# The feed-forward gate of a conditioned transformer block: half of the inner state copied out of PSUM beside the tanh and multiplied on GpSimd, and the attention's reciprocals kept in PSUM

## The chip, the cores and the metric

The kernel runs on one core of a Trainium2 chip. The metric is the device time of the whole program in microseconds. TensorE is written PE here, VectorE DVE, ScalarE ACT, GpSimd POOL, and SyncE, which issues the DMAs, SP. All data is fp32, except for a mask kept in bf16.

## The reference, cut to what matters

Eight sequences of 512 tokens, 256 channels wide, pass through an adaptive-norm transformer block with 16 heads of 16 channels and an additive attention bias, then an adapter with experts and a layer norm, a rotation of channel pairs, and a second adapter. The two places that the change touches:

```python
probs = jax.nn.softmax(scores, axis=-1)
ctx = jnp.einsum('bhqk,bhkd->bhqd', probs, v)
...
def _gelu2(x):
    return x * jax.nn.sigmoid(1.702 * x)
h = _ln(x) * g2 + beta2
ff = _gelu2(h @ W1 + b1) @ W2 + b2        # W1: 256 x 1024, W2: 1024 x 256
```

The kernel writes the sigmoid as a tanh: `sigmoid(1.702 z) = 0.5 * tanh(0.851 z) + 0.5`, with `z = h @ W1 + b1`. The softmax is normalised late: a column of ones beside each head's values gives the sum of the exponentials, and the context is multiplied by the sum's reciprocal.

## The kernel before, in words

Attention goes in 128 units, `(b, g, qt)`: one sequence, a group of four heads, 128 queries. Each unit loads four bias tiles of 128 x 512 by DMA (L909), and POOL adds the mask to each (L913). PE computes four tiles of scores into four PSUM banks (L921). DVE subtracts scores and bias and finds the row's extreme (L933), ACT takes the exp in place (L937). The probabilities are turned, half of them on PE (L972) with an eviction by ACT or DVE (L693), half on DVE (L948) with a DMA that puts the blocks in place (L957). After every second unit PE multiplies them with the values (L998) into a bank called `pv`.

From there DVE alone works: it transposes the 128 x 256 columns of `pv` into an SBUF tile `pvs` (L1011), takes the reciprocals of eight sums into an SBUF tile `inv` (L1020), multiplies the context by them into `zed` (L1021), and after two groups transposes that into `ctx` (L1028).

After eight units, half a sequence is finished (`finish`): the output projection, the feed-forward, two adapters. `feed_forward` takes 256 tokens at a time, and for the last half sequence of all 128 at a time. The 1024 inner channels go in eight chunks of 128, two to a group, so there are 68 groups in all, 60 of them 256 tokens wide. In each, PE writes two chunks into the two halves of one PSUM bank (L1053), ACT takes a tanh of each half into `sig` (L1062), POOL makes 0.5 t + 0.5 of both at once (L1065), and DVE multiplies that by the biased inner state, which it reads from the bank again (L1069). The product `gT` is the stationary operand of the second matmul (L1078).

The order of the work is not written by hand. Each step is a task with an engine and a cost, the buffers and tiles that it reads and writes, and a rank. `Plan.run` plays these tasks through in a model with their costs: a free engine takes the ready task of lowest rank. A task with costs for two engines goes to whichever is free, ACT first. What comes out is the order in which instructions are emitted, for PE, DVE, ACT, POOL and SP together; each engine then works through its own in that order, with semaphores between them. So a changed cost or dependency can shift the order of everything after it. Eight PSUM banks are split in two sets of four: `SC` for the scores, `BG` for all the rest, which may borrow from `SC`. There are 16 bias tiles, the room for four units.

```python
BG = Slots(banks[4:], SC)
BIAS = slots("bias", 16, [P, S])
GT = slots("gT", 1, [P, NF, 2 * P])
SIG = slots("sig", 2, [P, 2, 2 * P])
```

Of the kernel before, what the change touches and what calls it, by code (L numbers as in the profile page):

```python
# [11 lines left out]
F32 = mybir.dt.float32  # L12
# [3 lines left out]
AF = mybir.ActivationFunctionType  # L16
ALU = mybir.AluOpType
AX = mybir.AxisListType

P = 128  # L20
B, S, D, H, HD, FF = 8, 512, 256, 16, 16, 1024
# [3 lines left out]
NF = FF // P  # L25
# [13 lines left out]
C_BQ, C_BK, C_B1, C_G2, C_BETA2, C_DB, C_FREQ, N_COLS = 0, 4, 8, 16, 18, 20, 22, 23  # L39
# [5 lines left out]
PE, DVE, ACT, POOL, DMA = "PE", "DVE", "ACT", "POOL", "DMA"  # L45
# [193 lines left out]
def conditioned_sequence_kernel(  # L239
# [22 lines left out]
    nc = tc.nc  # L262
    const = ctx.enter_context(tc.tile_pool(name="const", bufs=1))
# [9 lines left out]
    def slots(name, count, shape, dtype=F32):  # L273
        return Slots([const.tile(shape, dtype, tag=f"{name}{i}", name=f"{name}{i}") for i in range(count)])
# [3 lines left out]
    BG = Slots(banks[4:], SC)  # L278
# [12 lines left out]
    PT = slots("pT", 2, [P, 4 * NT * 2 * P])  # L291
    TB = slots("tb", 2, [P, TURNED * S])
    PVS = slots("pvs", 2, [P, 2 * P])
    INV = slots("inv", 2, [P, 8])
    ZED = slots("zed", 2, [P, 8, 2, HD])
    CTX = slots("ctx", 2, [P, NC, 2 * P])
    HT = slots("hT", 2, [P, NC, 2 * P])
# [13 lines left out]
    cols = const.tile([P, N_COLS], F32, tag="cols", name="cols")  # L311
# [66 lines left out]
    plan = Plan()  # L378
# [8 lines left out]
    wq = const.tile([P, NC, NC, P], F32, tag="wq", name="wq")  # L387
    wk = const.tile([P, NC, NC, P], F32, tag="wk", name="wk")
    b1s = const.tile([P, NF], F32, tag="b1s", name="b1s")
    valid = const.tile([A, B], F32, tag="valid", name="valid")  # L390
    invalid = const.tile([A, B], F32, tag="invalid", name="invalid")
    expert_i = const.tile([1, B], I32, tag="expert_i", name="expert_i")
# [106 lines left out]
    def constants():  # L499
        plan.rank = -13.0  # L500

        further = Buffer(BG, lambda t: t[:, :8])
        plan(PE, 0.3, lambda: nc.tensor.matmul(
            further.t, shifted[:, :P], cols[:, :8], start=True, stop=True),
            [], [further], mode="full", at=3.9)

        def biases():
            nc.vector.tensor_tensor(
                bk,
                cols[:, C_BK : C_BK + NG].rearrange("p (c u) -> p c u", u=2)[:, :, 0],  # L510
                further.t[:, 4:8].rearrange("p (c u) -> p c u", u=2)[:, :, 1],
                ALU.add,
            )

            for u, src in enumerate((cols[:, C_BQ : C_BQ + NG], further.t[:, :4])):
                nc.vector.tensor_scalar(
                    bqh[:, u], src.rearrange("p (c u) -> p c u", u=2)[:, :, u],
                    halves[:, u : u + 1], None, ALU.mult,
                )

        plan(DVE, 0.6, biases, [further], ["bk", "bqh"], at=7.9)
        plan.rank = -1.9
        for n in (1, 2):
            plan(DMA, 0.45, lambda n=n: half_of(n, 1), [], [("raw", n, 1)], data=0.8)

        for c in range(NC):
            for n, w in ((1, wq), (2, wk)):

                def dense(n=n, w=w, c=c):
                    for k in range(NC):  # L530
                        src = first[:, n, k, c * 2 * P : (c + 1) * 2 * P]
                        src = src.rearrange("p (u j e) -> p u j e", u=2, e=32)[:, :, :, :HD]
                        dst = w[:, k, c, :].rearrange("p (j u d) -> p u j d", u=2, d=HD)
                        nc.gpsimd.tensor_copy(dst, src)

                plan.rank = -9.0 + 0.1 * n + 6.0 * c
                plan(POOL, 0.55, dense, [("raw", n, c)], [("w", n, c)], at=0 if c else 7.3 + 0.8 * n)


        for i, v_pad in enumerate(VP.tiles):  # L540

            def clear(v_pad=v_pad, i=i):
                nc.gpsimd.memset(v_pad, 0.0)
                ones = v_pad[:, : NT * H * (HD + 1)].rearrange("p (n e) -> p n e", e=HD + 1)
                nc.gpsimd.memset(ones[:, :, HD : HD + 1], 1.0)
                nc.gpsimd.memset(VT.tiles[i][:, NT * NG * TURNED * (HD + 1) :], 0.0)

            plan.rank = -10.0
            plan(POOL, 1.3, clear, [], [("ones", i)])
        plan.rank = 1.0  # L550

        def later():
            for hid in HID.tiles:
                nc.gpsimd.memset(hid[A:A1, :], 1.0)

        plan(POOL, 0.6, later, [], ["hid1"])

        plan(ACT, 0.25, lambda: nc.scalar.activation(
            b1s, cols[:, C_B1 : C_B1 + NF], AF.Copy, scale=0.851), [], ["b1s"], at=4.0)

    def late_weights():
        wo_rows = w_o.rearrange("(c u j e) n -> c j u e n", c=NC, u=2, e=32)
# [336 lines left out]
    def attention(u, n):  # L899
        b, g, qt = u  # L900
        c, par = divmod(g, 2)
        half, i = divmod(qt, 2)
# [64 lines left out]
        for j in range(turned, 4):  # L967
            ps = Buffer(BG, lambda t: t.rearrange("p (k q) -> p k q", k=NT))
# [15 lines left out]
        if g == 0:  # L984
            live[(b, half)] = Buffer(CTX)
        ctx_h = live[(b, half)]
        pv = Buffer(BG, lambda t: t[:, : 2 * P])

        def values():
            for kc in range(NT):  # L990
                for j in range(4):
                    at = ((j * NT + kc) * NG + g) * (HD + 1)
                    if j < turned:
                        pj = pT.t[:, : 8 * TURNED * P].rearrange(
                            "p (a h k c) -> p h k a c", a=8, h=TURNED, k=NT)[:, j, kc]
                    else:
                        pj = pT.t.rearrange("p (j k f) -> p j k f", j=4, k=NT)[:, j, kc]
                    nc.tensor.matmul(  # L998
                        pv.t[32 * j : 32 * j + 32, :],
                        (v_turn if j < turned else v_pad).t[:, at : at + 32],  # L1000
                        pj, start=(kc == 0), stop=(kc == NT - 1),
                    )
# [4 lines left out]
             + [(pT, a) for a in range(2) if turned], [pv], mode="col")  # L1007


        sb, inv = Buffer(PVS), Buffer(INV)  # L1010
        plan(DVE, 0.37, lambda: nc.vector.transpose(  # L1011
            sb.t.rearrange("p (i b c) -> p b i c", i=2, c=32),
            pv.t.rearrange("p (b i c) -> p b i c", i=2, c=32)), [pv], [sb])
        if par == 0:
            live[(b, half, c)] = Buffer(ZED)
        zed = live[(b, half, c)]

        def normalise():
            of = sb.t.rearrange("p (b e) -> p b e", e=32)
            nc.vector.reciprocal(inv.t, of[:, :, HD])  # L1020
            nc.vector.tensor_tensor(  # L1021
                zed.t[:, :, par, :], of[:, :, :HD],
                inv.t.unsqueeze(2).to_broadcast([P, 8, HD]), ALU.mult,
            )

        plan(DVE, 0.45, normalise, [sb], [inv, (zed, par)])
        if par == 1:
            plan(DVE, 0.35, lambda: nc.vector.transpose(  # L1028
                ctx_h.t[:, c, :], zed.t.rearrange("p b u d -> p (b u d)")),
                [(zed, 0), (zed, 1)], [(ctx_h, c)])  # L1030


    def feed_forward(res, rk, ts, store=None):
        hat = Buffer(TMP)
        at = {t: i for i, t in enumerate(ts)}
        n, w = len(ts), len(ts) * P
# [7 lines left out]
        gT = Buffer(GT) if store is None else store  # L1044
        for f2 in range(NF // 2):
            ps = Buffer(BG, lambda t: t.rearrange("p (i q) -> p i q", i=2))
            sg = Buffer(SIG)
            for i in range(2):
                f = 2 * f2 + i

                def hidden(i=i, f=f, ps=ps):
                    for c in range(NC):
                        nc.tensor.matmul(  # L1053
                            ps.t[:, i, :w], w1[:, c, f * P : (f + 1) * P], hT.t[:, c, :w],
                            start=(c == 0), stop=(c == NC - 1),
                        )

                plan(PE, 0.432 * n, hidden, [*hk, "w1"], [(ps, i)], mode="full")

            for i in range(2):  # L1060
                f = 2 * f2 + i
                plan(ACT, 0.155 + 0.1 * n, lambda i=i, f=f, ps=ps, sg=sg: nc.scalar.activation(  # L1062
                    sg.t[:, i, :w], ps.t[:, i, :w], AF.Tanh, bias=b1s[:, f : f + 1],
                    scale=0.851), [(ps, 0), (ps, 1), "b1s"], [(sg, i)])
            plan(POOL, 0.05 + 0.3 * n, lambda sg=sg: nc.gpsimd.tensor_scalar(  # L1065
                sg.t[:, :, :w], sg.t[:, :, :w], 0.5, 0.5, ALU.mult, ALU.add), [], [(sg, 0), (sg, 1)])
            for i in range(2):
                f = 2 * f2 + i
                plan(DVE, 0.14 + 0.13 * n, lambda i=i, f=f, ps=ps, sg=sg: nc.vector.scalar_tensor_tensor(  # L1069
                    gT.t[:, f, :w], ps.t[:, i, :w], cols[:, C_B1 + f : C_B1 + f + 1],  # L1070
                    sg.t[:, i, :w], ALU.add, ALU.mult), [(ps, i), (sg, i)], [(gT, f)])
        ps = Buffer(BG, lambda t: t.rearrange("p (i d) -> p i d", i=2))
        for i in range(n):
            for f0 in range(0, NF, 2):
# [317 lines left out]
```

## Time and profile before

| | |
|---|---|
| time of the runs | 930.76, 931.76, 935.42 us; median 931.76 |
| the profiled execution | 928.04 us, span 926.3 us |
| PE busy | 887.0 us, 96% of the span |
| DVE busy | 827.4 us, 89% |
| POOL busy | 755.3 us, 82% |
| ACT busy | 748.6 us, 81% |
| DMA engines, mean bandwidth | 236 GB/s |

The profile is of one execution. It counts an engine as busy while an instruction of its own runs; time in which an instruction waits at the head of its queue is idle time, and the profile names what ended it. Matmuls are pipelined, so PE can be shown as busy while it makes little progress. A row of the costliest groups gives the source line, the engine, the operation, output and inputs by name, their shapes, the count, and then the busy time in us, the mean duration of one in ns, and the idle time just before them with what ended it. A row of waits gives who waited for whom, the sum in us, how many times, and the longest.

### The profile page before, as it was taken

The page shows a single profiled execution, that of the slowest core. Times are in us where ns is not written, and L with a number is a line of the kernel's source. Part 1 is how long each engine was busy: PE and PEld are TensorE (multiplying, and loading weights), DVE is VectorE, ACT ScalarE, POOL GpSimd, SP SyncE. Part 2 cuts the span into 40 slices and gives each one's busy share as a digit, 9 for nine tenths or more (in the row PEclk, how much of TensorE's full clock was granted, in tenths as well). Part 3 has the DMA queues.
Part 4 walks back from the last instruction along what each step waited for, and adds up shares of the span by engine and source line. Part 5 has one row for each costly group of instructions (what it writes and reads, how often), then busy time and mean ns, then how long its engine had stood idle before and what let it go on. Part 6 is the DMA issues. An engine that isn't in the chain of part 4 may idle for free.

```text
span 926.3 us, 20595 instructions
## 1 busy us (share of the span) xinstructions
PE 887.0 (96%) x6430; PEld 576.8 (62%) x6430; DVE 827.4 (89%) x2197; ACT 748.6 (81%) x1357; POOL 755.3 (82%) x843
## 2 busy tenths in 40 slices
PE   9989999999999999999999999999998999999994
PEld 7546665656556666566656666566655666666682
DVE  4789888999989999989999998999998899999866
ACT  5976879878797778978889887987989779798653
POOL 8877999998687877998688887997879878999232
PEclk9999999999999998999999999999999999999997
DMA  9578786787867878787888869878796878998400
GB/s 316 172 242 271 233 266 194 219 275 246 290 174 245 264 218 283 213 266 244 244 263 246 283 204 288 246 227 270 235 310 197 258 250 274 290 301 263 108 23 23
DMA packets 163215, 218.55 MB, mean 236 GB/s; under 512 B 19167, under 2 KB 93961, under 8 KB 163106
## 3 DMA queue, kind: packets, MB, share of 16 engines
q1 hardware_dynamic: 163062, 217.22, 75.0%
q8 instruction: 51, 0.84, 0.4%
q14 instruction: 58, 0.48, 0.2%
q10 hardware_dynamic: 44, 0.02, 0.0%
HBM read 149.89 MB, written 4.24 MB: 166 GB/s over the span
## 4 chain that ended last, share of the span: by engine, by line
PE 51%; DVE 21%; ACT 12%; DMA 6%; issue 4%; POOL 3%; SPq 1%; DVEq 0%; POOLq 0%; ACTq 0%
PE bank L921 9%; PE bank L972 8%; PE bank L998 8%; PE bank L1078 7%; DVE bias L933 7%; PE bank L1053 6%; PE bank L811 5%; ACT bias L937 4%; DVE tb L948 3%; DMA pT<-tb 3%; DMA bias<-in_bias 3%; PE bank L759 2%; DVE st L701 2%; ACT sig L1062 1%; PE bank L410 1%
## 5 line engine op out<-in xcount | busy, mean ns | idle before, releaser
L913 POOL TENSOR_TENSOR bias<-bias,neg 128x512 f32<-128x512 f32 x512 | 582.0, 1164 | 84.8 <-DMA bias<-in_bias 57.1
L937 ACT ACTIVATE bias<-bias,low 128x512 f32<-128x512 f32 x512 | 341.9, 719 | 58.6 <-DVE low L933 57.6
L933 DVE CUSTOM_DVE_ANT_0 bias<-bank,bias 128x512 f32<-128x512 f32 x512 | 326.1, 679 | 21.2 <-PE bank L921 20.9
L972 PEld LDWEIGHTS bank<-shifted,bias 128*128 128x128 f32 x1120 | 126.1, 142 | 78.7 <-ACT bias L937 33.7
L972 PE MATMUL bank<-shifted,bias 128*128 128x128 f32 x1120 | 157.9, 280 | 12.7 <-DVE pT L693 5.1
L921 PE MATMUL bank<-kT,qz 32*128 32x512 f32 x1024 | 166.4, 642 | 1.5 <-DVE low L933 1.3
L948 DVE STREAM_TRANSPOSE tb<-bias 128x512 f32<-128x512 f32 x232 | 153.6, 689 | 10.8 <-DMA pT<-tb 6.3
L693 ACT COPY pT<-bank 128x512 f32<-128x512 f32 x221 | 121.4, 584 | 40.5 <-PE bank L972 39.6
L1053 PE MATMUL bank<-hT,w 128*128 128x256 f32 (+1 forms) x544 | 126.9, 375 | 0.5 <-DVE gT L1069 0.2
L998 PE MATMUL bank<-pT,v_pad 128*32 128x256 f32 x1120 | 124.3, 385 | 0.0
L1078 PE MATMUL bank<-w,gT 128*128 128x256 f32 x496 | 118.5, 384 | 0.5 <-DVE pT L693 0.3
L998 PE MATMUL bank<-pT,v_turn 128*32 128x256 f32 x928 | 112.7, 385 | 2.8 <-DMA pT<-tb 1.6
L1053 PEld LDWEIGHTS bank<-hT,w 128*128 128x128 f32 x544 | 93.8, 190 | 30.4 <-issue 12.2
L1078 PEld LDWEIGHTS bank<-w,gT 128*128 128x128 f32 x496 | 90.4, 190 | 25.5 <-issue 12.1
L921 PEld LDWEIGHTS bank<-kT,qz 32*128 32x128 f32 x1024 | 50.9, 183 | 54.2 <-issue 26.6
L998 PEld LDWEIGHTS bank<-pT,v_turn 128*32 128x32 f32 x928 | 50.2, 110 | 52.5 <-issue 9.8
L1065 POOL TENSOR_SCALAR sig<-sig 128x512 f32<-128x512 f32 (+1 forms) x68 | 40.3, 594 | 32.5 <-ACT sig L1062 29.0
L1062 ACT ACTIVATE sig<-bank,b1s 128x256 f32<-128x256 f32 (+1 forms) x136 | 55.1, 455 | 11.7 <-PE bank L1053 11.2
L998 PEld LDWEIGHTS bank<-pT,v_pad 128*32 128x32 f32 x1120 | 55.0, 110 | 5.9 <-ACT bias L937 1.5
L1069 DVE SCALAR_TENSOR_TENSOR gT<-bank,cols,sig 128x256 f32<-128x256 f32 (+1 forms) x128 | 53.8, 462 | 3.1 <-POOL sig L1065 2.8
L701 DVE BATCH_NORM_STATS2 st<-res 128x6 f32<-128x256 f32 x128 | 52.1, 407 | 1.6 <-DMA res<-in_x 0.2
L1021 DVE TENSOR_TENSOR zed<-pvs,inv 128x128 f32<-128x128 f32 x64 | 49.0, 766 | 2.2
(138 smaller groups left out, 1127.4 us busy)
## 6 DMA issues: line engine op xcount, KB each, us to landing
bias<-in_bias SPq DMA_DIRECT2D x512, 256.0 KB
pT<-tb SPq DMA_DIRECT2D x464, 128.0 KB
out<-res SPq DMA_DIRECT2D x15, 256.0 KB
res<-in_x SPq DMA_DIRECT2D x7, 512.0 KB
v_turn<-v_pad SPq DMA_DIRECT2D x32, 68.0 KB
m<-in_mask SPq DMA_DIRECT2D x8, 256.0 KB
mod<-ada_rows SPq DMA_DIRECT2D x8, 256.0 KB
w<-in_w SPq DMA_DIRECT2D x2, 1024.0 KB
```

The source lines that it names most:

```text
L693: nc.scalar.copy(*pair()) if e == ACT else nc.vector.tensor_copy(*pair())), r, w)
L701: plan(DVE, 0.43, lambda t=t, st=st: nc.vector.bn_stats(st.t, src.t[:, t, :]), [key], [st], at=at[i] if at else 0.0)
L913: plan(POOL, 1.12, lambda j=j: nc.gpsimd.tensor_tensor(dif[j].t, dif[j].t, negs[qt].t, ALU.add), [negs[qt]], [dif[j]])
L921: nc.tensor.matmul(sc[j].t, qz.t[strip, par, c, qs], kT.t[strip, c, :], start=True, stop=True,)
L933: plan(DVE, 0.61, lambda j=j: nc.vector.tensor_tensor_reduce(dif[j].t, sc[j].t, dif[j].t, -1.0, 3.0e38, ALU.add, ALU.min, low.t[:, j : j + ...
L937: plan(ACT, 0.61, lambda j=j: nc.scalar.activation(dif[j].t, dif[j].t, AF.Exp, bias=low.t[:, j : j + 1], scale=-1.0), [(low, j)], [dif[j]] ...
L948: plan(DVE, 0.62, lambda j=j: nc.vector.transpose(tb.t.rearrange("p (m h k c) -> h p k m c", m=4, h=TURNED, k=NT)[j], dif[j].t.rearrange(" ...
L972: nc.tensor.transpose(ps.t[:, kc, :], dif[j].t[:, kc * P : (kc + 1) * P], ident)
L998: nc.tensor.matmul(pv.t[32 * j : 32 * j + 32, :], (v_turn if j < turned else v_pad).t[:, at : at + 32], pj, start=(kc == 0), stop=(kc == N ...
L1053: nc.tensor.matmul(ps.t[:, i, :w], w1[:, c, f * P : (f + 1) * P], hT.t[:, c, :w], start=(c == 0), stop=(c == NC - 1),)
L1062: plan(ACT, 0.155 + 0.1 * n, lambda i=i, f=f, ps=ps, sg=sg: nc.scalar.activation(sg.t[:, i, :w], ps.t[:, i, :w], AF.Tanh, bias=b1s[:, f : ...
L1078: nc.tensor.matmul(ps.t[:, i, :], gT.t[:, f, i * P : (i + 1) * P], w2[:, f, :], start=(f == 0), stop=(f == NF - 1),)
```

## The change

Two edits.

In the attention, the reciprocals no longer have an SBUF tile. They go into eight unused columns of the `pv` bank, from where the multiplication reads them; the task that does so now holds the bank as well, so that it comes free one task later. Three planned costs of DVE in this part are raised a little.

In the feed-forward, a second pass over the bank is added for each chunk: 0.5 z, out of PSUM into `gT`, by ACT or by DVE as the planner finds (`half_out`); for this `b1h` holds half the bias. POOL's step becomes t + 1, and POOL multiplies it by 0.5 z in place, two chunks at a time. The product on DVE, L1069, is gone, and so is its second reading of the bank after POOL.

```diff
-    INV = slots("inv", 2, [P, 8])
...
+        plan(ACT, 0.25, lambda: nc.scalar.activation(
+            b1h, cols[:, C_B1 : C_B1 + NF], AF.Copy, scale=0.5), [], ["b1h"], at=4.0)
...
-        pv = Buffer(BG, lambda t: t[:, : 2 * P])
+        pv = Buffer(BG)
...
-        sb, inv = Buffer(PVS), Buffer(INV)
-        plan(DVE, 0.37, lambda: nc.vector.transpose(
+        sb = Buffer(PVS)
+        plan(DVE, 0.43, lambda: nc.vector.transpose(
...
-            nc.vector.reciprocal(inv.t, of[:, :, HD])
+            inv = pv.t[:, 2 * P : 2 * P + 8]
+            nc.vector.reciprocal(inv, of[:, :, HD])
             nc.vector.tensor_tensor(
-                zed.t[:, :, par, :], of[:, :, :HD],
-                inv.t.unsqueeze(2).to_broadcast([P, 8, HD]), ALU.mult,
+                zed.t[:, :, par, :], inv.unsqueeze(2).to_broadcast([P, 8, HD]),
+                of[:, :, :HD], ALU.mult,
             )
 
-        plan(DVE, 0.45, normalise, [sb], [inv, (zed, par)])
+        plan(DVE, 0.52, normalise, [sb, pv], [(pv, "inv"), (zed, par)])
...
+                def half_out(e, i=i, f=f, ps=ps):
+                    if e == ACT:
+                        nc.scalar.activation(
+                            gT.t[:, f, :w], ps.t[:, i, :w], AF.Identity,
+                            bias=b1h[:, f : f + 1], scale=0.5)
+                    else:
+                        nc.vector.tensor_scalar(
+                            gT.t[:, f, :w], ps.t[:, i, :w], cols[:, C_B1 + f : C_B1 + f + 1],
+                            0.5, ALU.add, ALU.mult)
+
+                plan({ACT: 0.155 + 0.1 * n, DVE: 0.14 + 0.13 * n}, 0.0, half_out,
+                     [(ps, 0), (ps, 1), "b1h"], [(gT, f)])
+            a0 = 2 * f2
             plan(POOL, 0.05 + 0.3 * n, lambda sg=sg: nc.gpsimd.tensor_scalar(
-                sg.t[:, :, :w], sg.t[:, :, :w], 0.5, 0.5, ALU.mult, ALU.add), [], [(sg, 0), (sg, 1)])
-            for i in range(2):
-                f = 2 * f2 + i
-                plan(DVE, 0.14 + 0.13 * n, lambda i=i, f=f, ps=ps, sg=sg: nc.vector.scalar_tensor_tensor(
-                    gT.t[:, f, :w], ps.t[:, i, :w], cols[:, C_B1 + f : C_B1 + f + 1],
-                    sg.t[:, i, :w], ALU.add, ALU.mult), [(ps, i), (sg, i)], [(gT, f)])
+                sg.t[:, :, :w], sg.t[:, :, :w], 1.0, None, ALU.add), [], [(sg, 0), (sg, 1)])
+            plan(POOL, 0.05 + 0.54 * n, lambda a0=a0, sg=sg: nc.gpsimd.tensor_tensor(
+                gT.t[:, a0 : a0 + 2, :w], sg.t[:, :, :w], gT.t[:, a0 : a0 + 2, :w],
+                ALU.mult), [(sg, 0), (sg, 1)], [(gT, a0), (gT, a0 + 1)])
```

More of the change, by code (lines that the diff above doesn't have):

```diff
@@ L389, in conditioned_sequence_kernel @@
     b1s = const.tile([P, NF], F32, tag="b1s", name="b1s")
+    b1h = const.tile([P, NF], F32, tag="b1h", name="b1h")
     valid = const.tile([A, B], F32, tag="valid", name="valid")
@@ L998, in values @@
                     nc.tensor.matmul(
-                        pv.t[32 * j : 32 * j + 32, :],
+                        pv.t[32 * j : 32 * j + 32, : 2 * P],
                         (v_turn if j < turned else v_pad).t[:, at : at + 32],
@@ L1007, in attention @@
              + [(pT, a) for a in range(2) if turned], [pv], mode="col")
-        sb, inv = Buffer(PVS), Buffer(INV)
-        plan(DVE, 0.37, lambda: nc.vector.transpose(
+        sb = Buffer(PVS)
+        plan(DVE, 0.43, lambda: nc.vector.transpose(
             sb.t.rearrange("p (i b c) -> p b i c", i=2, c=32),
-            pv.t.rearrange("p (b i c) -> p b i c", i=2, c=32)), [pv], [sb])
+            pv.t[:, : 2 * P].rearrange("p (b i c) -> p b i c", i=2, c=32)), [pv], [sb])
         if par == 0:
@@ L1019, in normalise @@
             of = sb.t.rearrange("p (b e) -> p b e", e=32)
-            nc.vector.reciprocal(inv.t, of[:, :, HD])
+            inv = pv.t[:, 2 * P : 2 * P + 8]
+            nc.vector.reciprocal(inv, of[:, :, HD])
             nc.vector.tensor_tensor(
-                zed.t[:, :, par, :], of[:, :, :HD],
-                inv.t.unsqueeze(2).to_broadcast([P, 8, HD]), ALU.mult,
+                zed.t[:, :, par, :], inv.unsqueeze(2).to_broadcast([P, 8, HD]),
+                of[:, :, :HD], ALU.mult,
             )
-        plan(DVE, 0.45, normalise, [sb], [inv, (zed, par)])
+        plan(DVE, 0.52, normalise, [sb, pv], [(pv, "inv"), (zed, par)])
         if par == 1:
-            plan(DVE, 0.35, lambda: nc.vector.transpose(
+            plan(DVE, 0.44, lambda: nc.vector.transpose(
                 ctx_h.t[:, c, :], zed.t.rearrange("p b u d -> p (b u d)")),
```

## The prediction

> **What bounds the kernel now.** I read the busy shares first, then the chain of work that ended last.
>
> ```profile
> PE 887.0 (96%) x6430; PEld 576.8 (62%) x6430; DVE 827.4 (89%) x2197; ACT 748.6 (81%) x1357; POOL 755.3 (82%) x843
> ...
> PE 51%; DVE 21%; ACT 12%; DMA 6%; issue 4%; POOL 3%; SPq 1%; DVEq 0%; POOLq 0%; ACTq 0%
> ```
>
> No engine alone sets the time. PE is busiest, but only 51% of the chain runs over it; a third runs over DVE and ACT, so time saved there counts in part. I weigh it by chain share over busy time: DVE 0.21 x 926.3 / 827.4 = 0.235, ACT 0.12 x 926.3 / 748.6 = 0.148. POOL has 3% of the chain, and what matters is how much more it can take. For that I took a stretch of six whole batches, 116 to 812 us: its busy times (columns: PE, PEld, DVE, ACT, POOL), then POOL's waits in it.
>
> ```profile
> sum 696.00, PE 677.82 PEld 434.66 DVE 646.71 ACT 587.73 POOL 596.06; mean PE 112.97 PEld 72.44 DVE 107.79 ACT 97.95 POOL 99.34
> ```
>
> ```profile
> POOL bias L913 <- DMA bias<-in_bias: 49.6, 42, 3.9
> POOL bias L913 <- DVE pvs L1011: 7.4, 2, 4.8
> POOL sig L1065 <- ACT sig L1062: 7.4, 10, 1.6
> POOL bias L913 <- DVE low L933: 6.8, 4, 4.1
> ```
>
> POOL is idle for 696 - 596 = 100 us there. Of that, 49.6 us it waits for bias tiles from DMA: it is ahead of its input, and this time more work can fill. The other 50 us are waits for other engines and gaps. So the free room is nearer 50 us than 100. Last, the groups that the change touches, and the rows that price it:
>
> ```profile
> L913 POOL TENSOR_TENSOR bias<-bias,neg 128x512 f32<-128x512 f32 x512 | 582.0, 1164 | 84.8 <-DMA bias<-in_bias 57.1 <-DVE pvs L1011 7.4 <-PE bank L921 7.1
> ...
> L1069 DVE SCALAR_TENSOR_TENSOR gT<-bank,cols,sig 128x256 f32<-128x256 f32 x120 | 51.5, 470 | 1.8 <-POOL sig L1065 1.6
> L1062 ACT ACTIVATE sig<-bank,b1s 128x256 f32<-128x256 f32 x120 | 49.9, 467 | 6.8 <-PE bank L1053 6.5
> L1021 DVE TENSOR_TENSOR zed<-pvs,inv 128x128 f32<-128x128 f32 x64 | 49.0, 766 | 2.2
> ...
> L888 POOL TENSOR_TENSOR res<-res,mod 128x512 f32<-128x512 f32 x32 | 40.7, 1274 | 0.6
> ```
>
> ```profile
> L1021 DVE TENSOR_TENSOR zed<-pvs,inv x64: 291/622/5882, 46.0 to 880.9; 128x128 f32<-128x128 f32 x64
> ```
>
> ```profile
> L1148 DVE TENSOR_TENSOR tmp<-bank,rot x64: 251/280/309, 146.3 to 914.5; 128x128 f32<-128x128 f32 x64
> ```
>
> The last two (minimum/median/maximum ns) are one operation of one size on DVE. L1148 reads one input from PSUM and never exceeds 309 ns; L1021 reads both from SBUF and goes from 291 ns to 5.9 us.
>
> **Part 1: context's reciprocals in PSUM.** Counts are from the built instruction order. 64 reciprocals write 8 columns into the free half of the pv bank instead of SBUF, and L1021 reads them there. The trace shows the stretching but not its cause. The Trainium skill gives one (SBUF — State Buffer, "Who interferes with whom": a DVE instruction with two SBUF inputs contends with a GpSimd instruction that reads SBUF; whichever came second stands still until the first is done). With one PSUM input L1021 should cost what L1148 does: 64 x (766 - 279) = 31.2 us off DVE. The ends are 0 (another cause) and 64 x (766 - 251) = 33 us; I take 31.2. The reciprocal stays at 203 ns (write target changed, 8 columns; bound 150 to 260, 64 x 0.06 = 4 us either way). The pv bank stays taken longer by 203 + 279 = 0.48 us, 64 times; DVE's own later work is not delayed, only PE's reuse of one of the four working banks. Hidden as long as another bank is free: 0 here, at most 3 us, as much again as PE waits today for L1011 and L1021 together (3.1 us).
>
> **Part 2: the gate on GpSimd.** Removed: 136 products on DVE (120 x 0.470 off its row plus 16 narrow ones, 4.7 us) = 56.2 us. Added: 136 half copies out of PSUM. The built order puts 83 on DVE (73 wide, 10 narrow) and 53 on ACT (47 and 6). No row has this form; for DVE L1069 is nearest (same shape, one operand from PSUM, a scalar per partition): 73 x 0.470 + 10 x 0.345 = 37.8 us (bounds 0.41, a plain PSUM add of this width at L857, and 0.54, L802's 0.80 us less half its columns: 33 to 43). For ACT the tanh itself is nearest: 47 x 0.467 + 6 x 0.364 = 24.1 us (up to 0.56 by L745: 28.6). The planner also shifts evictions: 7 of hT and 2 of pT go from ACT to DVE, 2 of eu the other way: DVE +5.3, ACT -4.5.
>
> - DVE: -31.2 - 56.2 + 37.8 + 5.3 = -44.3 us, at 0.235: **-10.4 us**.
> - ACT: +24.1 - 4.5 = +19.6 us, at 0.148: **+2.9 us**. The one new bias instruction at the start (0.2 us) hides under the loads.
> - PE: no instruction more or less; its order and SP's are re-planned throughout, with the same counts. An order can be luckier or not: 0, bounds -4 and +4.
>
> **POOL** gets 68 products of two SBUF tiles. Here a rule and a row differ. The Trainium skill (GPSIMD Engine Reference, "4.1 Engine selection") tells one to keep elementwise work off GpSimd, where two-input operations are about twice as slow, and its measured 2.6 cycles an element make 512 x 2.6 / 1.2 = 1109 ns, an estimate. The trace has 1164 ns where one input is bf16 (L913) and 1274 ns where both are f32 (L888), as here. By the page 60 wide ones cost 66.5 us, by the row 76.4; the row decides. Eight narrow ones at 0.7 (0.64 half of it, 0.83 by L1065's ratio 405/620) add 5.6: **+82.0 us, POOL at 837 of 926**. In the six batches it is 48 x 1.274 = 61.2 us against 49.6 us of room: 11.6 us too many, which must lengthen those batches unless its other waits shrink: **+11.6 us**. Queued behind each product on POOL are the bias additions L913, for which DVE's L933 and then every exp and transpose wait. If the cover (POOL's lead over L933) is gone, all further POOL waits count whole.
>
> **The new wait.** In the diff tanh and half copy depend only on the matmuls, and where they fall on two engines they seem to run side by side. The Trainium skill speaks against it (PSUM — Partial Sum Buffer, "PSUM bank collisions raise a hardware error": no two engines may touch one bank and quadrant at once, two readers included, so accesses are to be guarded by bank). The built order does guard them: in 51 of 68 groups ACT and DVE take turns on the bank, with 98 waits for each other, 53 on ACT and 45 on DVE. The trace of before has no such handover, since there DVE reads after POOL. Side by side the waits would cost 0. In turns, one is the other's 0.47 us plus two handovers of about 0.09 (ACT's tanh to POOL, 858.39 to 858.47): 0.65 us with the whole queue behind it standing, exps on ACT, L933 on DVE. 20 on each engine follow its own access at once, whole price; I halve the rest, which often arrive late anyway. ACT 20 x 0.65 + 33 x 0.33 = 23.9 us at 0.148; DVE 20 x 0.65 + 25 x 0.33 = 21.3 us at 0.235: **+8.5 us** (0 to 11).
>
> **What the bank gains.** Before, it is held over two tanhs, POOL's step and two products; after, until the copies end, without POOL. The trace has PE waiting about 4 us for L1069 over all lines, so at most 4: **-2 us**. **Tail:** with one token tile, turns in place of two tanhs (4 x 0.36 + 0.3 against 0.62) precede the last output matmuls: **+1.2 us**.
>
> Sum: -10.4 + 2.9 + 11.6 + 8.5 - 2 + 1.2 = +11.8 us. On the profiled execution's own 928.0 us (span 926.3 and 1.7 around it) that is 939.8. It was quicker than the timed runs, whose median is 931.8, so I forecast 931.8 + 11.8 = **943.5 us**.
>
> **Rivals.**
> *DVE's relief decides (faster).* POOL's product goes wholly into its DMA waits, the turns fall where the queues were late anyway, and DVE's -10.4 stands: about 922 us. For it: 49.6 us of POOL waits, DVE at 93% in the six batches. Against it: the 11.6 us excess. It decides if POOL's lead over L933 survives, that is if its other 50 us of idle time give up 12.
> *Nothing to see.* Gains and losses off PE cancel under its 97%: 931. For it PE's share, against it a chain that is half elsewhere.
> *POOL becomes the bound.* Its waits other than for bias tiles stay: 171 us idle less 57.1 is 114; with 837 busy that is 951, +25 on the span: 957. For it: in-order POOL now waits for turns too. Against it: a late engine finds its inputs ready.
> *The reciprocal edit does nothing.* L1021 stays at 766 ns: DVE loses its 31.2 x 0.235 = 7.3 us gain, 951.
>
> **How the numbers follow.** Forecast, within 934 to 950: 0.42. Faster rival: 0.15. Same: 0.20. POOL-bound or the reciprocal without effect: 0.23. A measurement of this kernel tells about 0.5% (4.7 us) from no change. Faster 0.15; same 0.20; slower 0.65. The range reaches from the upper part of the faster case to the POOL-bound end: 925 to 958.
>
> **What would show it.** L1021 near 0.28 us with no long ones; DVE near 783 us, ACT near 768, POOL near 837; L913's waits for DMA well below 57 us, and L933 waiting for POOL, now 0.3 us; waits between the tanh and the half copies that sum to 20 us or more on each engine. I am wrong if POOL still waits 50 us for DMA, or if these turns cost under 5 us: then it is faster.

## The result, and the profile after

The changed kernel takes 960.89 us (median of three runs, 960.68 to 962.59) against 931.76 us before: 1.0308 of it, with a 95% interval of 1.0261 to 1.0355. It is slower, as forecast, but by 29 us where the forecast had 12, and above its range, which ended at 958. The profiled execution took 962.59 us, span 960.8 us.

The busy shares, and the shares of the chain of work that ended last, of the kernel after:

```profile
PE 890.1 (93%) x6430; PEld 575.5 (60%) x6430; DVE 791.7 (82%) x2151; ACT 764.7 (80%) x1404; POOL 888.8 (93%) x911
...
PE 34%; ACT 19%; POOL 17%; DVE 10%; DMA 10%; issue 6%; SPq 3%; POOLq 0%; DVEq 0%; ACTq 0%
```

DVE and ACT are within 9 us of what the prediction had (783 and 768). POOL is not: 888.8 where it had 837, and its part of the chain has grown from 3% to 17%. The six whole batches, which took 696 us before, last from 120 to 840 us. Their busy times after:

```profile
sum 720.00, PE 676.28 PEld 431.93 DVE 623.28 ACT 598.49 POOL 697.79; mean PE 112.71 PEld 71.99 DVE 103.88 ACT 99.75 POOL 116.30
```

POOL is now busy for 697.8 of 720 us, 97%, more than PE. PE's own work is the same as before (678 us there); it is only spread over 24 us more. Which instruction of POOL's it is, the groups after tell (each row: busy us and mean ns behind the bar, then idle time before):

```profile
L1082 POOL TENSOR_SCALAR sig<-sig 128x512 f32<-128x512 f32 x60 | 89.7, 1495 | 10.6 <-ACT sig L1065 7.2 <-DVE tb L950 1.4 <-DVE pT L695 0.3
L1084 POOL TENSOR_TENSOR gT<-sig,gT 128x512 f32<-128x512 f32 x60 | 76.7, 1278 | 4.8
...
L1075 DVE TENSOR_SCALAR gT<-bank,cols 128x256 f32<-128x256 f32 x73 | 33.9, 478 | 28.8 <-ACT sig L1065 20.9 <-PE bank L1056 6.6 <-ACT gT L1071 0.9
...
L1071 ACT ACTIVATE gT<-bank,b1h 128x256 f32<-128x256 f32 x47 | 22.3, 476 | 0.0
```

The new product, L1084, costs what its neighbour row had promised (1278 ns, 1274 forecast), and the half copies too (478 and 476 ns, forecast 470 and 467). The surprise is L1082. It is the old step 0.5 t + 0.5 made into t + 1, one arithmetic operation where there were two, and it takes 1495 ns. The prediction left it at its old price.

The waits after, in us, times and longest, with the bias addition (L915, formerly L913) and the subtraction that needs it (L935, formerly L933):

```profile
DVE bias L935 <- POOL bias L915: 36.8, 55, 3.3
...
DVE gT L1075 <- ACT sig L1065: 21.4, 31, 1.8
...
ACT sig L1065 <- DVE gT L1075: 18.1, 32, 1.1
...
POOL bias L915 <- DMA bias<-in_bias: 5.1, 5, 2.7
```

POOL no longer waits for bias tiles (57 us before, 5 now, and those outside the six batches): it is late, not early. DVE waits 36.8 us for it, where before there was only this:

```profile
DVE bias L933 <- POOL bias L913: 0.3, 1, 0.3
```

The two middle lines above are the turns on the bank. The multiplication by the reciprocals has lost its long cases (min/median/max ns):

```profile
L1024 DVE TENSOR_TENSOR zed<-bank,pvs x64: 290/291/292, 47.1 to 911.7; 128x128 f32<-128x128 f32 x64
```

### The profile page after: what moved, and what is told of

Same layout as the page of the kernel before. It is cut to its first block, busy times and chain, and to the rows that moved or that the text cites. A ratio compares the mean times of both kernels' runs of the same rounds, so it can differ in the third digit from the quotient of the medians.

```text
span 960.8 us, 20783 instructions
## 1 busy us (share of the span) xinstructions
PE 890.1 (93%) x6430; PEld 575.5 (60%) x6430; DVE 791.7 (82%) x2151; ACT 764.7 (80%) x1404; POOL 888.8 (93%) x911
## 4 chain that ended last, share of the span: by engine, by line
PE 34%; ACT 19%; POOL 17%; DVE 10%; DMA 10%; issue 6%; SPq 3%; POOLq 0%; DVEq 0%; ACTq 0%
POOL bias L915 10%; PE bank L923 6%; PE bank L1093 6%; ACT bias L939 6%; DMA bias<-in_bias 6%; PE bank L974 5%; PE bank L1000 4%; PE bank L1056 4%; DVE bias L935 3%; PE bank L813 2%; DMA pT<-tb 2%; POOL sig L1082 2%; ACT sig L1065 2%; ACT pT L695 2%; ACT bank L725 2%
## 5 line engine op out<-in xcount | busy, mean ns | idle before, releaser
L915 POOL TENSOR_TENSOR bias<-bias,neg 128x512 f32<-128x512 f32 x512 | 577.7, 1162 | 10.6 <-DMA bias<-in_bias 5.1
L935 DVE CUSTOM_DVE_ANT_0 bias<-bank,bias 128x512 f32<-128x512 f32 x512 | 330.2, 681 | 59.1 <-POOL bias L915 36.8
L974 PE MATMUL bank<-shifted,bias 128*128 128x128 f32 x1120 | 160.2, 280 | 21.4 <-ACT bias L939 8.6
L1093 PE MATMUL bank<-w,gT 128*128 128x256 f32 x496 | 121.2, 387 | 5.7 <-POOL gT L1084 5.0
L1082 POOL TENSOR_SCALAR sig<-sig 128x512 f32<-128x512 f32 (+1 forms) x68 | 96.5, 1419 | 15.7 <-ACT sig L1065 11.1
L1084 POOL TENSOR_TENSOR gT<-sig,gT 128x512 f32<-128x512 f32 (+1 forms) x64 | 79.6, 1243 | 5.2
L1065 ACT ACTIVATE sig<-bank,b1s 128x256 f32<-128x256 f32 (+1 forms) x136 | 60.5, 459 | 24.5 <-DVE gT L1075 18.1
L923 PEld LDWEIGHTS bank<-kT,qz 32*128 32x128 f32 x1024 | 48.0, 184 | 52.9 <-issue 26.6
L1075 DVE TENSOR_SCALAR gT<-bank,cols 128x256 f32<-128x256 f32 (+1 forms) x77 | 35.2, 471 | 29.5 <-ACT sig L1065 21.4
L725 ACT ACTIVATE bank<-res,rstd 128x256 f32<-128x256 f32 x64 | 36.5, 570 | 25.1 <-POOL rstd L712 23.9
```

Source lines behind the costliest of these rows:

```text
L915: plan(POOL, 1.12, lambda j=j: nc.gpsimd.tensor_tensor(dif[j].t, dif[j].t, negs[qt].t, ALU.add), [negs[qt]], [dif[j]])
L923: nc.tensor.matmul(sc[j].t, qz.t[strip, par, c, qs], kT.t[strip, c, :], start=True, stop=True,)
L935: plan(DVE, 0.61, lambda j=j: nc.vector.tensor_tensor_reduce(dif[j].t, sc[j].t, dif[j].t, -1.0, 3.0e38, ALU.add, ALU.min, low.t[:, j : j + ...
L974: nc.tensor.transpose(ps.t[:, kc, :], dif[j].t[:, kc * P : (kc + 1) * P], ident)
L1093: nc.tensor.matmul(ps.t[:, i, :], gT.t[:, f, i * P : (i + 1) * P], w2[:, f, :], start=(f == 0), stop=(f == NF - 1),)
```

## The experiments

Every ratio is against the kernel before on the same chip, with its 95% interval behind it. Where two experiments are compared, I take the difference of their ratios times 931.8 us; the intervals of both then leave some 3 to 8 us either way.

### The step of POOL with both operations again

```diff
-                sg.t[:, :, :w], sg.t[:, :, :w], 1.0, None, ALU.add), [], [(sg, 0), (sg, 1)])
+                sg.t[:, :, :w], sg.t[:, :, :w], 1.0, 1.0, ALU.mult, ALU.add), [], [(sg, 0), (sg, 1)])
```

This computes the same, as 1.0 t + 1.0, in the same order of instructions as the changed kernel.

> The changed kernel with POOL's t + 1 written as two operations, 1.0 t + 1.0 (multiply, add), as the kernel before wrote 0.5 t + 0.5; values and order of instructions stay. Theory A (POOL is the bound, and its one-operation step at 1.50 us, which the prediction had at 0.62, is the term that was mis-sized): L1082 near 0.62 us, POOL from 889 to about 833 us, waits for bias tiles come back, and the time falls to what the prediction had summed up, 935 to 948. Theory B (the turns of ACT and DVE on one bank are what costs): POOL falls likewise, but the time stays at 955 to 961.

926.05 us, ratio 0.994 (0.9915 to 0.9964). The page, and then the group of the step:

```profile
PE 876.3 (95%) x6430; PEld 570.7 (62%) x6430; DVE 789.7 (85%) x2151; ACT 761.9 (82%) x1404; POOL 832.5 (90%) x911
```

```profile
L1082 POOL TENSOR_SCALAR sig<-sig 128x512 f32<-128x512 f32 x60 | 37.1, 619 | 21.4 <-ACT sig L1065 16.7 <-DVE pT L695 3.0 <-DVE low L935 0.5
```

The step is back at 619 ns, and POOL's total falls by 56.3 us (60 x 0.876 + 8 narrow ones x 0.44) to 832.5, next to the 837 of the prediction. The whole slowdown is gone with it: (1.0308 - 0.994) x 931.8 = 34.3 us for one dropped multiplication. The step and POOL's total are those of theory A; the time is below its 935 to 948, so something else of the prediction's sum was too dear. Six batches of this kernel:

```profile
sum 696.00, PE 667.12 PEld 428.50 DVE 622.36 ACT 596.41 POOL 655.57; mean PE 111.19 PEld 71.42 DVE 103.73 ACT 99.40 POOL 109.26
```

They last 696 us again, with 40 us of POOL's time unused. The waits between POOL, ACT and DVE in this kernel, to compare with later ones:

```profile
POOL sig L1082 <- ACT sig L1065: 21.7, 22, 4.2
DVE gT L1075 <- ACT sig L1065: 18.0, 29, 1.1
...
ACT sig L1065 <- DVE gT L1075: 15.0, 30, 1.1
```

### Each part of the change alone

The attention edit alone, on the kernel before (its core):

```diff
-            nc.vector.reciprocal(inv.t, of[:, :, HD])
+            inv = pv.t[:, 2 * P : 2 * P + 8]
+            nc.vector.reciprocal(inv, of[:, :, HD])
...
-        plan(DVE, 0.45, normalise, [sb], [inv, (zed, par)])
+        plan(DVE, 0.52, normalise, [sb, pv], [(pv, "inv"), (zed, par)])
```

> The kernel before with the attention edit alone (reciprocals in PSUM, with its planned costs). Theory A (two SBUF inputs made DVE's L1021 stand still for POOL; its 31 us count with the weight of DVE in the chain): the multiplication at 0.29 us flat, DVE from 827 to about 796 us, time 922 to 928. Theory B (it was off the path, or the longer hold of the pv bank takes it back): DVE falls likewise, time 930 to 936.

921.23 us, 0.9893 (0.9834 to 0.9953): 1.1% or 10.0 us faster, just below theory A's range. DVE falls to 792.8 us, by 34.6, of which the multiplication is 64 x (766 - 291) = 30.4. Its durations in this kernel:

```profile
L1021 DVE TENSOR_TENSOR zed<-bank,pvs x64: 291/291/293, 45.7 to 871.0; 128x128 f32<-128x128 f32 x64
```

The feed-forward edit alone is the changed kernel with that attention edit undone, its planned costs too:

```diff
-            inv = pv.t[:, 2 * P : 2 * P + 8]
-            nc.vector.reciprocal(inv, of[:, :, HD])
+            nc.vector.reciprocal(inv.t, of[:, :, HD])
...
-        plan(DVE, 0.52, normalise, [sb, pv], [(pv, "inv"), (zed, par)])
+        plan(DVE, 0.45, normalise, [sb], [inv, (zed, par)])
```

> The changed kernel with the attention edit undone (reciprocals in SBUF again): the feed-forward edit alone. Theory A (POOL bounds the changed kernel): L1021 stands still for an even busier POOL, over 0.77 us in the mean, and the time is that of the changed kernel or up to 8 us more, 958 to 970. Theory B (the longer held pv bank is part of the loss): below 955.

1014.79 us, 1.0871 (1.0791 to 1.0952), far above both theories: the two parts together are far better than the second alone. The multiplication there, and a stretch of the timeline around its worst case (start us, duration us, engine and instruction):

```profile
L1024 DVE TENSOR_TENSOR zed<-pvs,inv x64: 291/842/9034, 45.9 to 962.7; 128x128 f32<-128x128 f32 x64
```

```profile
806.36 0.20 DVE L1023 RECIPROCAL inv<-pvs 128x8 f32<-128x8 f32 x1
806.60 9.03 DVE L1024 TENSOR_TENSOR zed<-pvs,inv 128x128 f32<-128x128 f32 x1
...
807.45 1.26 POOL L891 TENSOR_TENSOR res<-res,mod 128x512 f32<-128x512 f32 x1
...
808.68 5.58 POOL L916 TENSOR_TENSOR bias<-bias,neg 128x512 f32<-128x512 f32 x5
...
814.23 1.25 POOL L891 TENSOR_TENSOR res<-res,mod 128x512 f32<-128x512 f32 x1
815.66 0.45 DVE L1031 STREAM_TRANSPOSE ctx<-zed 128x256 f32<-128x256 f32 x1
...
816.16 2.93 PE L762 MATMUL bank<-wo,ctx 128*128 128x256 f32 x6 [7.34 <-DVE ctx L1031]
...
816.74 1.33 ACT L940 ACTIVATE bias<-bias,low 128x512 f32<-128x512 f32 x2 [7.27 <-DVE low L936]
```

DVE's 0.29 us of work lasts 9.03 us, until POOL pauses at 815.5. The seven POOL instructions shown (1.26 + 5.58 + 1.25 us) follow without a gap on the one that was running when DVE came. PE's output projection and ACT's exp stand for 7.3 us behind DVE. From 814 on the granted TensorE clock is halved (below, each row is a stretch, its length, the busy time of PE, PEld, DVE, ACT and POOL, and then, third from the end, the granted share of the clock):

```profile
804.00:814.00 10.00, 4.82 (x58) 2.63 (x50) 9.48 (x6) 4.24 (x6) 10.00 (x10) 1.00 0.84 266
814.00:824.50 10.50, 8.34 (x27) 5.47 (x28) 9.79 (x25) 3.21 (x6) 2.40 (x4) 0.51 0.01 2
```

Such cases are few. The usual one is this, from the kernel before:

```profile
167.44 1.17 POOL L913 TENSOR_TENSOR bias<-bias,neg 128x512 f32<-128x512 f32 x1
...
167.74 1.02 DVE L1021 TENSOR_TENSOR zed<-pvs,inv 128x128 f32<-128x128 f32 x1
...
168.58 0.66 POOL L1065 TENSOR_SCALAR sig<-sig 128x512 f32<-128x512 f32 x1
```

The multiplication ends 0.15 us after the POOL instruction that was running when it came, and POOL goes straight on. In the trace of the kernel before 48 of the 64 end like that, 39 of them while POOL goes straight on; 15 are not delayed, and one, of 5.88 us, outlasts five further POOL instructions. Beyond 64 x 0.29 us the multiplication takes 30.4 us there and 62.8 here (mean 766 and 1273 ns). The cases under 2 us make 25 us of that in both kernels; those over 2 us make 5.6 before (one) and 37.4 here (five). So it is the long ones that have grown. Why a few stand over several POOL instructions, when most stand over one, stays open.

The same with POOL's step as multiply and add:

```diff
-                sg.t[:, :, :w], sg.t[:, :, :w], 1.0, None, ALU.add), [], [(sg, 0), (sg, 1)])
+                sg.t[:, :, :w], sg.t[:, :, :w], 1.0, 1.0, ALU.mult, ALU.add), [], [(sg, 0), (sg, 1)])
```

> The feed-forward edit alone, with POOL's step in two operations: reciprocals in SBUF. With the one-operation step this pair cost 1014.8 us, 54 more than with the reciprocals in PSUM. Theory A (DVE's two-input multiplication stands still until POOL's unbroken run of instructions ends, and runs get long where POOL is full): with POOL less full the long waits of 7 to 9 us thin out, time 933 to 955. Theory B (the feed-forward edit is bad in itself once the reciprocals are in SBUF, whatever POOL does): above 970.

969.14 us, 1.0431 (1.0398 to 1.0464), between the two theories: the form of POOL's step costs 41 us in this pair. Undoing the edit also undoes its planned costs and frees the bank earlier, so the order of everything differs; the next pair keeps it.

### The reciprocals in SBUF, all else as it was

The first takes the changed kernel with the multiply-and-add step, the second the kernel before with the attention edit. Order, planned costs and the time for which the bank is held stay; only where eight numbers lie is changed (and the two inputs of the multiplication change places, as in the kernel before):

```diff
+    INV = [const.tile([P, 8], F32, tag=f"inv{i}", name=f"inv{i}") for i in range(2)]
...
-            inv = pv.t[:, 2 * P : 2 * P + 8]
+            inv = INV[sb.slot]
```

> The changed kernel with POOL's step in two operations and its order of instructions untouched, but the reciprocals written to and read from an SBUF tile: nothing but the place of one small operand differs from the run at 926.05 us. Theory A (the second SBUF input makes DVE wait for POOL's runs): the multiplication goes from 0.29 to about 1.0 us in the mean, with single waits of several us, and the time to 945 to 970. Theory B (the loss of the feed-forward edit alone, 969 us, came from its own re-planned order): 924 to 932.

953.12 us, 1.0203 (1.0118 to 1.0287), against 0.994 with the reciprocals in PSUM: theory A. Their place is worth 0.0263 x 931.8 = 24.5 us. DVE is busy 831.6 us instead of 789.7, so a saved us of DVE is worth 24.5 / 41.9 = 0.58 us. The multiplication, 1.00 us in the mean, is:

```profile
L1025 DVE TENSOR_TENSOR zed<-pvs,inv x64: 291/705/6580, 45.9 to 909.8; 128x128 f32<-128x128 f32 x64
```

It takes over 5 us three times. In this trace and in that of the feed-forward edit alone there are eight such cases; each leaves PE idle for 4.4 to 7.3 us, and from within that time or just behind it the granted clock is halved for 3.4 to 10.2 us. The profiled execution has a mean granted clock of 0.972 over 956.9 us, the one with the reciprocals in PSUM 0.986 over 927.1. So 26.8 us of clock are missing against 13.0, and by an estimate from these numbers at most 14 of the 30 us between the two executions can be the clock's, if PE set the time throughout. No run parts the clock from the standing itself.

> The kernel before with the attention edit's planned costs, its longer hold of the pv bank and its order of instructions, but the reciprocals in an SBUF tile. Theory A (the gain of the attention edit alone, 1.1%, is DVE's waiting for POOL): 929 to 936. Theory B (it is the order that the new costs bring): 919 to 924.

941.3 us, 1.0104 (1.0073 to 1.0135), against 0.9893: 19.7 us in the kernel before, and for 33.2 us less of DVE (826.0 and 792.8) again 0.59 us each. The time is above both theories: 1% slower than the kernel before itself, which has the reciprocals in SBUF too. So the new planned costs, the order that comes out of them or the longer hold of the bank cost 9.7 us there, and the 10.0 us of the attention edit are what is left of 19.7. In the feed-forward pair it is the other way round (0.0228, some 21 us, better with the new ones than with the old). Which of the three it is stays open.

### The one-operation step in the kernel before

```diff
-                sg.t[:, :, :w], sg.t[:, :, :w], 0.5, 0.5, ALU.mult, ALU.add), [], [(sg, 0), (sg, 1)])
+                sg.t[:, :, :w], sg.t[:, :, :w], 1.0, None, ALU.add), [], [(sg, 0), (sg, 1)])
```

The factor 0.5 of the gate is left out.

> The kernel before with POOL's step written as one operation, t + 1 (the factor 0.5 of the gate is left out, so its feed-forward is twice as large); order unchanged. Theory A (the form itself is slow): the step takes 1.50 us here too, POOL goes from 755 to about 811 us, and since POOL had 50 to 57 us of waits for bias tiles the time moves little, 931 to 939. Theory B (it is slow only in the company of the new product): 0.62 us and 931.

955.7 us, 1.0278 (1.0207 to 1.035), much more than expected. The step in this kernel, then the waits:

```profile
L1065 POOL TENSOR_SCALAR sig<-sig x68: 847/1495/1534, 101.9 to 922.5; 128x512 f32<-128x512 f32 x60, 128x256 f32<-128x256 f32 x8
```

```profile
POOL bias L913 <- DMA bias<-in_bias: 56.0, 35, 5.4
...
DVE gT L1069 <- POOL sig L1065: 26.9, 38, 1.7
```

The duration is the form's own: nothing of the change is needed for it. POOL has 56 us of idle time before bias tiles, which is as much as the step grew (755.3 to 810.4), and yet the time went up by 25.9 us. The idle time was not where the work was added. The step lies between ACT's tanh and DVE's product, and before, DVE had waited for it this long:

```profile
DVE gT L1069 <- POOL sig L1065: 2.8, 5, 1.2
```

The growth of 24 us is no less than the 20.7 us by which the profiled execution became longer (948.7 against 928.0), while DVE's waits for bias additions only go from 0.3 to 2.1 us. That these waits are the cause is argued from the rows; no run takes them away alone.

### Which forms are slow

Each of the four groups of a pass of the kernel before gets another form of the step. The first and the third leave out the factor 0.5, the second the addition of 0.5.

```diff
+                if f2 == 0:
+                    nc.gpsimd.tensor_scalar(t, t, 1.0, None, ALU.add)
+                elif f2 == 1:
+                    nc.gpsimd.tensor_scalar(t, t, 0.5, None, ALU.mult)
+                elif f2 == 2:
+                    nc.gpsimd.tensor_scalar(t, t, 1.0, 0.0, ALU.add, ALU.add)
+                else:
+                    nc.gpsimd.tensor_scalar(t, t, 0.5, 0.5, ALU.mult, ALU.add)
```

> The kernel before with POOL's step in four forms, one for each pair of chunks of a half sequence: t + 1 alone, 0.5 t alone (the offset 0.5 is left out there, and the factor 0.5 in the pair before, so the feed-forward's values are not the reference's), (t + 1) + 0 as two additions, and 0.5 t + 0.5 as before. Theory A (any one-operation form is slow): 1.50, 1.50, 0.62, 0.62 us. Theory B (it is addition that is slow): 1.50, 0.62, 1.50, 0.62. Theory C (only multiply-and-add has a quick form): 1.50, 1.50, 1.50, 0.62.

The lines of the four, in that order (min/median/max ns):

```profile
L1068 POOL TENSOR_SCALAR sig<-sig x17: 852/1497/1510, 105.8 to 931.4; 128x512 f32<-128x512 f32 x15, 128x256 f32<-128x256 f32 x2
...
L1070 POOL TENSOR_SCALAR sig<-sig x17: 854/1503/1509, 109.5 to 932.2; 128x512 f32<-128x512 f32 x15, 128x256 f32<-128x256 f32 x2
...
L1072 POOL TENSOR_SCALAR sig<-sig x17: 1085/1939/1957, 111.0 to 935.8; 128x512 f32<-128x512 f32 x15, 128x256 f32<-128x256 f32 x2
...
L1074 POOL TENSOR_SCALAR sig<-sig x17: 407/620/666, 120.0 to 938.3; 128x512 f32<-128x512 f32 x15, 128x256 f32<-128x256 f32 x2
```

An addition alone takes 1.50 us, a multiplication alone 1.50, two additions 1.94, and multiply-and-add 0.62 us. That is theory C, but for the two additions, which it had at 1.50. It is neither the number of operations nor the addition: of the forms tried, multiply-and-add is the quick one. Why, no run shows. A single run of this kernel took 964.06 us; no comparison of times rests on it.

### The turns on the bank

Both start from the changed kernel with the multiply-and-add step. In the first, the two half copies of a group are one task on one engine, after both tanhs, so that the bank changes hands once at most; 39 handovers are left of 98.

```diff
-                plan({ACT: 0.155 + 0.1 * n, DVE: 0.14 + 0.13 * n}, 0.0, half_out,
-                     [(ps, 0), (ps, 1), "b1h"], [(gT, f)])
+            plan({ACT: 0.31 + 0.2 * n, DVE: 0.28 + 0.26 * n}, 0.0, halves_out,
+                 [(ps, 0), (ps, 1), "b1h", (sg, 0), (sg, 1)], [(gT, 2 * f2), (gT, 2 * f2 + 1)])
```

> The changed kernel with POOL's step in two operations, and both half copies of a group as one task after both tanhs, on one engine: 39 handovers of a bank between ACT and DVE in place of 98. Theory A (taking turns on the bank costs about what the prediction put on it, 8.5 us at 98 handovers): waits between tanh and half copies fall from 33 to under 20 us, and the time by 3 to 6 us, to 920 to 923. Theory B (the turns cost next to nothing, what is left is POOL's product): 924 to 929.

913.51 us, 0.9847 (0.9821 to 0.9874): below theory A's 920 to 923, and better than both kernels. Waits of this kernel:

```profile
DVE gT L1077 <- ACT sig L1065: 12.8, 11, 3.7
...
POOL sig L1084 <- ACT sig L1065: 7.5, 3, 4.3
```

ACT no longer waits for DVE's copies (15.0 us with the turns), DVE waits for ACT 12.8 us instead of 18.0, and POOL for the tanh 7.5 instead of 21.7, since both tanhs now come first. The gain of 0.0093 x 931.8 = 8.7 us belongs to fewer handovers, to the earlier tanh and to the new order that comes with them; the run doesn't part them.

In the second, every half copy is on ACT, and none is handed over:

```diff
-                plan({ACT: 0.155 + 0.1 * n, DVE: 0.14 + 0.13 * n}, 0.0, half_out,
+                plan({ACT: 0.155 + 0.1 * n}, 0.0, half_out,
```

> The changed kernel with POOL's step in two operations and all 136 half copies on ACT: no handover at all, ACT up by about 39 us to 800, DVE down by about 37 to 752. By the chain's weights (ACT 0.15, DVE 0.24, turns 8.5 us) theory A gives 926 - 8.5 + 6 - 9, near 915 to 921; theory B (ACT is now as much on the path as DVE, and turns are cheap) 924 to 932.

918.85 us, 0.9892 (0.9864 to 0.9921), in theory A's range. ACT rises only to 776.3 us, for the planner moves evictions to DVE, which stands at 769.8. Having no handover gains 4.5 us on the 98, and 39 with the work shared out gain 8.7; the intervals of neighbours among the three touch, so only the ends of the row are clearly apart.

### What the order alone does

Planned costs shift the order of everything, so two kernels change such a cost and nothing else. The first gives POOL's product its measured price in the one-handover version, the second changes the price of POOL's step in the kernel before a little:

```diff
-            plan(POOL, 0.05 + 0.54 * n, lambda a0=a0, sg=sg: nc.gpsimd.tensor_tensor(
+            plan(POOL, 0.06 + 0.61 * n, lambda a0=a0, sg=sg: nc.gpsimd.tensor_tensor(
```

```diff
-            plan(POOL, 0.05 + 0.3 * n, lambda sg=sg: nc.gpsimd.tensor_scalar(
+            plan(POOL, 0.04 + 0.29 * n, lambda sg=sg: nc.gpsimd.tensor_scalar(
```

> The one-handover kernel (913.51 us) with POOL's product planned at what it measured, 1.28 us in place of 1.13; no work differs, the order is planned anew. Theory A (the planner's picture of POOL matters where POOL is 91% busy): 905 to 911. Theory B (it is only another order): 910 to 920.

> The kernel before with POOL's step planned at 0.62 us in place of 0.65: the same instructions and sizes in another order. It tells how much a re-planned order alone moves the time. If an order is nearly neutral, 929 to 935; if it is a lottery of the size of the effects studied, up to 10 us from 931.8 either way.

916.32 us, 0.9806 (0.9723 to 0.989), no difference from the one-handover version that the intervals show (theory B); and 931.86 us, 1.0006 (0.9977 to 1.0035), none from the kernel before. These two re-orderings are neutral, which says that not every new order moves the time; it doesn't clear the others.

## Why the prediction was right or wrong

**The step that failed: POOL.** "+82.0 us, POOL at 837 of 926" priced the new product and silently kept POOL's own step, L1065, at its old duration, since one operation in place of two looked no dearer. It costs 56 us more, 48 x 0.876 = 42 us of it in the six batches. Its own working would then have had POOL at 893 (888.8 measured) and another 42 us beyond the room: 943.5 + 42 = 985, slower than what came. The step cost 34.3 us of these 42, and most of the remaining distance is the next term. No row of the trace showed the one-operation form. The half copies, which had no row either, were bounded from both sides; this step was not.

**The second: what part 1 is worth.** Its 31.2 us of DVE were right for the kernel before (the multiplication at 0.291, the reciprocal at 0.211 us), and weighing them by DVE's share of the chain, 0.235, made 7.3 us of them. In runs of the same order the place of the reciprocals is worth 24.5 us in the changed kernel and 19.7 in the one before, 0.58 and 0.59 of the DVE time saved. The weight was too small: the share is an average over all of DVE's time, and behind a multiplication that stands, ACT and PE stand too, and the clock falls around the longest. Why it is just 0.6 no run shows. In the changed kernel the amount was too small as well: L1021's old mean was taken as what the edit saves, although a busier POOL was part of the same change, and without the edit the multiplication would have gone to 1.0 us in the same order. The rest of part 1 was put at nothing, and in the kernel before its planned costs, order and longer hold cost 9.7 us. That is why the attention edit alone, at 10.0 us, came near the 7.3: two errors that cancel. The rival "the reciprocal edit does nothing" falls with the multiplication's row after.

The first two errors also cancel in part. With POOL's step at the price that the prediction gave it, the kernel takes 926, and not 943.5.

In one table, by the terms of the forecast, in us:

| term | forecast | measured |
|---|---|---|
| reciprocals in PSUM | -7.3 | -24.5 |
| POOL's step as one operation | 0 | +34.3 |
| all the rest: copies, product, turns, bank, tail | +19.1 | +18.9 |
| sum | +11.8 | +28.7 |

The measured terms are differences along one path of kernels, so their sum has to be the result. What each says is its own. The third is the kernel with the multiply-and-add step and the reciprocals in SBUF, and its interval is 11 to 27 us. That it falls on the forecast must be called luck: none of its terms was measured by itself, and it also holds the attention edit's planned costs, order and hold, which the forecast had at nothing and which cost 9.7 us in the kernel before and gain some 21 in the feed-forward pair.

One sum of the prediction does not come out as written: 120 x 0.470 + 4.7 is 61.1 us, not 56.2. The 56.2 is the row's busy time, 51.5, plus 4.7, and that is the figure to use, since neighbouring instructions overlap a little. The copies' busy times came out as forecast, 37.2 us on DVE (37.8) and 24.5 on ACT (24.1).

**The turns.** That they are there was right, and their size nearly: 21.4 us on DVE (21.3 forecast) and 18.1 on ACT (23.9). The price of 8.5 us for all 98 stands beside 8.7 us for doing away with 59 of them and giving POOL its tanh earlier, and 4.5 for having none with the copies all on ACT. So what the turns alone cost stays open.

**The rivals.** "POOL becomes the bound" put 957 and came nearest, with a right picture, 97% in the six batches and DVE waiting, and a wrong sum: it had 837 us busy and 114 idle, and it is 889 and 72. "DVE's relief decides" (922) is what the change would nearly have been with the multiply-and-add step (926). "Nothing to see" (931) falls with the 960.89.

**What would show it.** The prediction said it would be wrong, and the kernel faster, if POOL still waited 50 us for DMA or if the turns cost under 5 us. The first did not come, and the second no run tells. Of its marks the waits came (5.1 us for bias tiles, 36.8 for POOL before the subtraction, 21.4 on DVE between tanh and copy), except that ACT's 18.1 stay below the 20 named. It named POOL's 837 us as the mark of its own step, and that mark is the one that failed.

## What to carry to other kernels

Price every instruction form that an edit introduces, also the one that looks simpler than the one it replaces, from a row of that very form; where there is none, measure it first. Idle time of an engine covers added work only if it lies where the work is added: here 56 us of it, before bias tiles, did not cover 55 us added between ACT's tanh and DVE's product. Where DVE and GpSimd work side by side, look for DVE instructions with two SBUF inputs: moving eight columns to PSUM was worth 0.6 us for each us of DVE it saved, where the chain's share had promised 0.235. And where two engines read one bank, try letting it change hands once; here that went with 8.7 us.

## What the runs showed of the hardware that was not expected

On GpSimd, a tensor_scalar over 128 x 512 fp32 took 0.62 us as multiply-and-add, 1.50 us as one addition or one multiplication and 1.94 us as two additions.

A DVE multiplication with two SBUF inputs stood, in 48 of 64 cases of the kernel before, until 0.15 us after the end of the GpSimd instruction that was running when it came. The Trainium skill (SBUF — State Buffer, "Who interferes with whom") has the second one stand until the first is done, which for one bias addition would be 1.16 us at most. That fits these cases. It does not fit the one of 5.88 us in the same kernel or the five of 5.9 to 9.03 us with the feed-forward edit alone, which outlasted five to seven further GpSimd instructions. These six ended when GpSimd paused; one of 6.46 us, with the reciprocals in SBUF and all else as it was, ended while it went on. With one input in PSUM, 64 of 64 took 290 to 293 ns.

A long stall cost clock besides. Each of the eight multiplications of over 5 us in two of these traces left PE idle for 4.4 to 7.3 us, and from within that time or just behind it the granted TensorE clock was halved for 3.4 to 10.2 us (0.51 in the 10.5 us shown above).
